# Moving six of eight token transposes from TensorE to DRAM plus VectorE in a Strassen-tiled transformer block

## The chip, the cores and the metric

The kernel runs on one core of one Trainium2 chip, in fp32. The metric is the device time of one execution in microseconds. Three runs of the kernel before gave a median of 853.25 us, from 852.59 to 854.26. The profile was taken from one more execution, which took 852.22 us; its instructions cover a span of 850.4 us.

The engines are named as in the profile: PE is TensorE (PEld its weight loads), DVE is VectorE, ACT is ScalarE, POOL is GpSimd, SP is SyncE, which only issues DMAs here.

## The reference

Four sequences (B = 4) of 512 tokens with 512 features go through two residual blocks. Every `layernorm` is without weights.

```
x = x + layernorm(attn(layernorm(x)))
x = x + layernorm(ffn(layernorm(x)))

attn(x):  i, f, g = x Wi', x Wf', x Wg'            # 512 -> 512 each
          gate = sigmoid(f);  v = silu(i) * (1 - gate)
          o[t] = gate[t] * o[t-1] + v[t]           # a scan over the tokens
          o = rmsnorm(o) * gnorm_w * g * sigmoid(g)
          return o Wo'
ffn(x):   h = silu(x W1') * (x W3')                # 512 -> 2048
          return fwht(h) W2'                       # Hadamard transform, 2048 -> 512
```

The Hadamard transform is applied to W2 instead of to h, once, at the start.

## The kernel before

All large products are done with one level of the Strassen-Winograd scheme: both operands are cut into 2 x 2 blocks, and seven products P1 to P7 of sums of blocks take the place of eight. `ORDER` lists them in the order in which PE runs them: P1, P2, P6, P5, P7, P3, P4. Their results go into three PSUM banks X, Y and Z, and X and Z are added into again by a later product, so a product has to wait until the state that the one before it left in its bank was read out (by ACT, `nc.scalar.copy`, or by DVE, `nc.vector.tensor_add`, in `seven`). One product is 8 matmuls of 128 x 256 columns.

The left operand's sums S1, S2, S4 (S3 takes the place of A21) are made by `combine_left`, the right operand's T1, T2, T4 (T3 in place of B12) by `combine_right`, both on DVE.

The work of a sequence b is

* `normalize(b, "a")`: statistics on DVE, the power -1/2 on POOL, the scaling on ACT (L234); the result `xn` has the tokens on the partitions;
* `transpose(b, "a")`: 16 PE transposes of 128 x 128 with the identity (L281) into four PSUM banks, two copies out by DVE (L288), two by ACT (L286), then `combine_right`; the result `xt` has the features on the partitions and holds the seven right blocks. It is the moving operand of all products with weights;
* three attention units `attn_unit(b, u)`: u = 0 and 1 make half of i and f each and scan; u = 2 makes g and the gated output `og`, a left operand;
* `attn_out(b)`: the product of `og` with Wo (tile y), then the norm of the output, and `normalize` and `transpose` of the new x under the name "f";
* eight FFN units `ffn_unit(b, m)`, 256 hidden features each, and `ffn_out` after every second, which adds into the tile `f`; the last one ends with the output norm.

The order on PE and on SP is the order of the program text, by hand (`tc.manual_schedule`). So that PE never waits for the results of a unit, the products of `attn_out`, `ffn_out` and of the one-time W2 transform are put in a list `fill`, and `run` takes one of them after every product (dense) or after four of the seven. The order on DVE, ACT and POOL is made by a scheduler, which knows priorities: `tc.high_priority(offset=URGENT)` pulls PSUM reads forward, `SOON` is weaker; `behind("P3")` puts work on DVE behind the PSUM read of the last P3.

Weights stream through five buffers (`stream`, w1, w3, wi, wf, wg) and four (`stream2`, wo, w2). In the first sequence each weight tile is read from its input, combined on DVE, used, and written to DRAM with its sums (`kept`, on the POOL queue); later sequences read that back (`again`). Wo is prepared once, by `prepare_wo`: two tiles, four loads on SP (L496), four scalings by `gnorm_w` on DVE (L503), sums, write-back. Its first use is `attn_out(0)`, whose first product is put after P5 of `attn_unit(1, 0)`.

Each SP load waits in the queue for its buffer, for the DMA eight before it, and for what it reads, and everything behind it waits too. The tile `wide` has three buffers, shared by `xn`, `y` and `f`; `xt` has two.

The eight calls of `transpose` stand at these places of the span: (0,"a") at 11.9 us, (1,"a") at 62.3, (0,"f") at 118.0, (2,"a") and (1,"f") together at 281.5, (3,"a") and (2,"f") together at 473.1, (3,"f") at 672.9.

## Time and profile before

| | |
|---|---|
| median of three runs | 853.25 us |
| the profiled execution | 852.22 us, its span 850.4 us |
| PE busy | 825.3 us, 97% of the span |
| PEld, DVE, ACT, POOL busy | 709.5, 453.5, 263.3, 60.6 us |
| transposes on PE (L281) | 128, in groups of 16 that take 1.91 us |
| their PSUM copies on DVE and ACT | 16 and 16, medians 0.68 and 0.59 us |
| DMA | 159.05 MB, 187 GB/s over the span |
| median time to landing, 896 KB weight tile | 6.2 us |

Times in the timeline are from the span's start. A line of the timeline gives the start, the duration, the engine, the source line, the operation, the output and the inputs with their shapes, how many instructions of this kind follow one another, and in brackets how long the engine had been idle and what ended that. A product of 8 matmuls is shown with 1.89 us, but the next one starts 1.73 us after it, since matmuls overlap.

### The profile page before, as it was taken

The numbers are of one execution on the slowest core, as the hardware profiler recorded it, in microseconds if no ns is written. First come the engines' busy times: TensorE is split into PE (matmuls) and PEld (weight loads), VectorE is DVE, ScalarE is ACT, GpSimd is POOL, SyncE is SP. The second block draws the span as 40 slices with busy tenths as digits, with TensorE's granted clock in tenths as the row PEclk, the third lists the DMA queues.
The fourth block names the chain that finished last, engine by engine and source line by source line (L and its number), as shares of the span: only waits on it lengthen the run. The fifth ranks groups of instructions, "written<-read, shape, count | busy, mean of one in ns | idle before, by whom it ended". The sixth has DMA issues, their size and how long they took to land.

```text
span 850.4 us, 9880 instructions
## 1 busy us (share of the span) xinstructions
PE 825.3 (97%) x3808; PEld 709.5 (83%) x3808; DVE 453.5 (53%) x903; ACT 263.3 (31%) x386; POOL 60.6 (7%) x102
## 2 busy tenths in 40 slices
PE   6999989999999999999999999999999999999995
PEld 4778868888888888888888888888888888888884
DVE  6457686755663656537433645737334534633445
ACT  4454362433221225225321222423221211222111
POOL 4110110111110001002000000101000000100000
PEclk9999999999999999999999999999999999999998
DMA  9995376677788224826325222844251632625101
GB/s 315 412 344 212 119 264 231 222 272 272 283 297 304 87 87 158 373 95 240 136 95 209 94 87 93 316 160 174 87 214 44 261 151 110 224 86 217 64 23 49
DMA packets 53598, 159.05 MB, mean 187 GB/s; under 512 B 4272, under 2 KB 29488, under 8 KB 53552
## 3 DMA queue, kind: packets, MB, share of 16 engines
q1 hardware_dynamic: 46544, 121.71, 39.1%
q0 software_dynamic: 7008, 36.71, 10.9%
q8 instruction: 30, 0.49, 0.2%
q14 instruction: 16, 0.13, 0.0%
HBM read 120.66 MB, written 37.75 MB: 186 GB/s over the span
## 4 chain that ended last, share of the span: by engine, by line
PE 59%; issue 9%; DVE 4%; DMA 1%; ACT 1%; POOL 1%; SPq 0%; POOLq 0%; DVEq 0%
PE X_f L333 20%; PE Z_f L333 10%; PE X_po L466 9%; PE Z_po L466 5%; PE Y_f L333 5%; PE X_a L333 3%; PE Y_po L466 2%; PE X_y L419 2%; PE Z_a L333 1%; PE Z_y L419 1%; DMA s_w<-w 1%; PE Y_a L333 1%; DVE x L267 1%; DVE f L318 1%; DMA w<-in_W_dram 1%
## 5 line engine op out<-in xcount | busy, mean ns | idle before, releaser
L333 PE MATMUL X_f<-xt_f,w 128*128 128x256 f32 x1024 | 242.1, 380 | 2.4 <-DVE xt_f L288 1.2
L333 PEld LDWEIGHTS X_f<-xt_f,w 128*128 128x128 f32 x1024 | 193.7, 190 | 33.8 <-issue 3.8
L320 ACT COPY d_f<-X_f 128x512 f32<-128x512 f32 x96 | 56.1, 584 | 300.3 <-PE X_f L333 275.9
L333 PE MATMUL Z_f<-xt_f,w 128*128 128x256 f32 x512 | 121.1, 379 | 0.0
L466 PE MATMUL X_po<-w,ht 128*128 128x256 f32 x512 | 120.9, 379 | 0.2 <-DVE f L318 0.2
L333 PEld LDWEIGHTS Z_f<-xt_f,w 128*128 128x128 f32 x512 | 97.2, 190 | 15.1 <-issue 1.0
L466 PEld LDWEIGHTS X_po<-w,ht 128*128 128x128 f32 x512 | 97.2, 190 | 13.8 <-DVE f L318 0.6
L318 DVE TENSOR_TENSOR f<-X_po,f 128x512 f32<-128x512 f32 x52 | 35.8, 688 | 95.2 <-PE X_po L466 95.2
L348 DVE TENSOR_TENSOR ht<-d_f 128x1024 f32<-128x1024 f32 x32 | 39.1, 1221 | 73.9 <-ACT d_f L442 54.7
L466 PE MATMUL Z_po<-w,ht 128*128 128x256 f32 x256 | 60.6, 379 | 0.5 <-DVE f L318 0.5
L333 PE MATMUL Y_f<-xt_f,w 128*128 128x256 f32 x256 | 60.5, 379 | 0.0
L333 PEld LDWEIGHTS Y_f<-xt_f,w 128*128 128x128 f32 x256 | 48.6, 190 | 8.3 <-issue 1.2
L466 PEld LDWEIGHTS Z_po<-w,ht 128*128 128x128 f32 x256 | 48.6, 190 | 7.5 <-DVE f L318 0.9
L320 ACT COPY d_a<-X_a 128x512 f32<-128x512 f32 x36 | 21.0, 584 | 91.5 <-PE X_a L333 75.4
L214 POOL TENSOR_TENSOR rs_f<-rs_f,power 128x2 f32<-128x2 f32 x16 | 14.6, 915 | 482.3 <-DVE rs_f L211 461.5
L318 DVE TENSOR_TENSOR d_f<-Z_f,d_f 128x512 f32<-128x512 f32 x32 | 22.0, 689 | 26.4 <-PE Z_f L333 26.4
L333 PE MATMUL X_a<-xt_a,wi 128*128 128x256 f32 x128 | 33.3, 382 | 2.1 <-DVE xt_a L288 1.9
L318 DVE TENSOR_TENSOR d_f<-X_f,d_f 128x512 f32<-128x512 f32 x32 | 22.1, 690 | 24.9 <-PE X_f L333 24.9
L442 ACT ACTIVATE d_f<-d_f 128x1024 f32<-128x1024 f32 x32 | 33.8, 1055 | 0.9
L333 PE MATMUL X_a<-xt_a,wf 128*128 128x256 f32 x128 | 32.8, 379 | 0.0
L333 PE MATMUL X_a<-xt_a,wg 128*128 128x256 f32 x128 | 30.7, 382 | 2.3 <-DVE d_a L318 1.6
L318 DVE TENSOR_TENSOR f<-Z_po,f 128x512 f32<-128x512 f32 x28 | 19.3, 689 | 24.4 <-PE Z_po L466 24.4
(148 smaller groups left out, 995.5 us busy)
## 6 DMA issues: line engine op xcount, KB each, us to landing
w<-s_w SPq DMA_DIRECT2D x80, 896.0 KB, 6.2
s_w<-w POOLq DMA_DIRECT2D x24, 896.0 KB, 4.6
w<-in_W_dram SPq DMA_DIRECT2D x32, 256.0 KB, 5.6
wi<-s_wi SPq DMA_DIRECT2D x6, 896.0 KB, 9.4
wf<-s_wf SPq DMA_DIRECT2D x6, 896.0 KB, 6.6
wg<-s_wg SPq DMA_DIRECT2D x6, 896.0 KB, 5.4
wo<-s_wo SPq DMA_DIRECT2D x6, 896.0 KB, 9.3
w2p<-in_W_dram SPq DMA_DIRECT2D x8, 512.0 KB, 7.5
```

The costliest lines, as they stand in the source:

```text
L214: nc.gpsimd.tensor_tensor(r, r, power_t[:, 0:n], ALU.pow)
L267: nc.vector.scalar_tensor_tensor(x_t, y[:, i, t, :], r[:, t : t + 1], x_t, ALU.mult, ALU.add)
L318: read[what] = nc.vector.tensor_add(to, ps[which], to)
L320: nc.scalar.copy(to, ps[which])
L333: nc.tensor.matmul(ps[:, n, :], w[:, a, c, :], xt[:, bb, c, :], start=first and n == 0 and c == 0, stop=c == 1, skip_group_check=True,)
L348: nc.vector.tensor_mul(to.rearrange("p (t k) f -> p k t f", t=2), a.rearrange("p k (t f) -> p k t f", t=2), b2.rearrange("p k (t f) -> p k ...
L419: nc.tensor.matmul(ps[:, t, :], og[:, a, c, ts(t, P)], w[c][:, bb, :], start=first and t == 0 and c == 0, stop=c == 1, skip_group_check=True,)
L442: nc.scalar.activation(d[:, 0], d[:, 0], AF.Silu)
L466: nc.tensor.matmul(ps[:, t, :], hts[b, m][:, a, ts(t, P)], w[m][:, bb, :], start=first and t == 0 and m == ms[0], stop=m == ms[-1], skip_g ...
```

## The change

`normalize_tiles` writes the normalized tokens to DRAM, two token tiles (512 KB) per DMA on the POOL queue, except for (0,"a") and (0,"f"), which keep the transposes on PE. `load_fold` reads them back on the SP queue in four DMAs, each with 128 features of all tokens, to 32 partitions: partition 32 i + q holds, of the tokens 32 g + q, the features 128 i to 128 i + 127. In that layout `transpose_fold` needs only 32 x 32 block transposes: four DVE instructions with 512 elements per partition, each of which reads every fourth element, and then `combine_right` as before. To match, feature 4 p + c goes to partition p, block c; so weight rows are loaded with `(p c)` in place of `(c p)`, and the remaining PE transposes take columns with a step of four. Wo and W2, whose rows are not features of `xn`, stay as they were.

The six moved transposes are also issued earlier in the program: (1,"a") is loaded before `attn_unit(0, 2)` and transposed in it, ahead of `prepare_wo`; (2,"a"), (3,"a") and (3,"f") are loaded before FFN unit 6 and transposed before unit 7; (1,"f") and (2,"f") are loaded before attention unit 1 and transposed before unit 2.

```diff
-                in_=src[:, cols].rearrange("(c p) f -> p c f", p=P),
+                in_=src[:, cols].rearrange("(p c) f -> p c f", p=P),
...
+    ON_TENSOR = ("a", 0), ("f", 0)
...
+        if (name, b) not in ON_TENSOR:
+            if (name, b) not in xnd:
+                xnd[name, b] = scratch.tile(
+                    [NT, P, D], F32, tag=f"xn_{name}_{b}", name=f"xnd_{name}_{b}"
+                )
+            nc.gpsimd.dma_start(
+                out=xnd[name, b][i0 : i0 + n].rearrange("t p d -> p t d"),
+                in_=t[:, i0 : i0 + n, :],
+            )
...
-                    nc.tensor.transpose(pt[c][:, h, ts(i % 2, P)], xn[:, i, ts(c, P)], ident)
+                    nc.tensor.transpose(pt[c][:, h, ts(i % 2, P)], xn[:, i, c::ND], ident)
...
+    def load_fold(b, name):
+        folds[name, b] = t = work.tile(
+            [P, T // 32, P], F32, tag="wide", name=f"fold_{name}_{b}", bufs=3
+        )
+        rows = xnd[name, b].rearrange("t p d -> (t p) d")
+        for i in range(4):
+            nc.sync.dma_start(
+                out=t[ts(i, 32)],
+                in_=rows[:, ts(i, P)].rearrange("(g q) k -> q g k", q=32),
+            )
+
+    def transpose_fold(b, name):
+        fold = folds.pop((name, b)).rearrange("p (h g) k -> p h g k", h=2)
+        xt = work.tile([P, 7, 2, H], F32, tag="xt", name=f"xt_{name}_{b}", bufs=2)
+        with tc.high_priority(offset=SOON):
+            for c in range(ND):
+                to = xt[:, B11 : B12 + 1 : B12 - B11] if c < 2 else xt[:, B21 : B22 + 1]
+                nc.vector.transpose(
+                    to[:, :, c % 2, :].rearrange("p h (g q) -> p h g q", q=32),
+                    fold[:, :, :, c::ND],
+                )
+            combine_right(xt, nc.vector)
+        xts[name, b] = xt
...
     load_attn_w(1, 0)
+    load_fold(1, "a")
     attn_unit(0, 2)
+    with behind("P7"):
+        transpose_fold(1, "a")
     with behind("P3"):
         prepare_wo()
-    transpose(1, "a")
...
+            if m == 6 and not last:
+                load_fold(*((b + 2, "a") if b + 2 < B else (b + 1, "f")))
+            if m == NU - 1 and not last:
+                transpose_fold(*((b + 2, "a") if b + 2 < B else (b + 1, "f")))
             ffn_unit(b, m, b == 0)
...
-            transpose(b + 2, "a")
-            transpose(b + 1, "f")
...
+                if u == 1:
+                    load_fold(b + 1, "f")
+                if u == 2:
+                    transpose_fold(b + 1, "f")
                 attn_unit(b + 2, u)
...
-            transpose(b + 1, "f")
```

More of the change, by code (lines that the diff above doesn't have):

```diff
@@ L216, in scales @@
         return r, nb
-    xns = {}
+    xns, xnd = {}, {}
+    ON_TENSOR = ("a", 0), ("f", 0)
     def normalize_tiles(b, name, i0, n):
@@ L288, in transpose @@
                     nc.vector.tensor_copy(to[:, :, c % 2, :], pt[c])
+            combine_right(xt, nc.vector)
+        xts[name, b] = xt
+    folds = {}
+    def load_fold(b, name):
[18 more added lines that the diff above has]
+                )
             combine_right(xt, nc.vector)
```

## The prediction, made before the changed kernel ran

> **What bounds the kernel now.** I read the page's busy shares and slices first, then the chain, then PE's timeline at the eight transposes.

> ```profile
> PE 825.3 (97%) x3808; PEld 709.5 (83%) x3808; DVE 453.5 (53%) x903; ACT 263.3 (31%) x386; POOL 60.6 (7%) x102
> PE   6999989999999999999999999999999999999995
> DMA  9995376677788224826325222844251632625101
> PE 59%; issue 9%; DVE 4%; DMA 1%; ACT 1%; POOL 1%; SPq 0%; POOLq 0%; DVEq 0%
> ```

> PE bounds every stage after the first 21 us; DMA is full only in the first three slices (to 64 us). So what leaves PE counts in full, unless PE then waits elsewhere. The groups by shape and PE's timeline price the transposes:

> ```profile
> L281 PE MATMUL pt_f<-ident,xn_f 128*128 128x128 f32 x64 | 7.9, 273 | 0.1
> L281 PE MATMUL pt_a<-ident,xn_a 128*128 128x128 f32 x64 | 7.6, 273 | 0.0
> 281.46 1.91 PE L281 MATMUL pt_a<-ident,xn_a 128*128 128x128 f32 x16
> 283.21 1.91 PE L281 MATMUL pt_f<-ident,xn_f 128*128 128x128 f32 x16
> 284.96 1.03 PE L333 MATMUL X_a<-xt_a,wi 128*128 128x256 f32 x4
> ```

> One transpose takes PE 283.21 - 281.46 = 1.75 us, and here nothing more. At 62 us it also waits for copies, and there DVE is busy with Wo (mixed timeline):

> ```profile
> 61.37 0.87 DVE L503 TENSOR_SCALAR wo<-wo,gn 128x512 f32<-128x512 f32 x2
> 62.28 1.91 PE L281 MATMUL pt_a<-ident,xn_a 128*128 128x128 f32 x16
> 62.48 0.59 ACT L320 COPY d_a<-X_a 128x512 f32<-128x512 f32 x1 [4.59 <-PE X_a L333]
> 63.10 1.91 ACT L375 ACTIVATE d_a<-d_a 128x2048 f32<-128x2048 f32 x1
> 64.72 1.28 DVE L288 COPY xt_a<-pt_a 128x512 f32<-128x512 f32 x2
> 65.46 1.13 PE L333 MATMUL X_a<-xt_a,wi 128*128 128x256 f32 x4 [1.26 <-DVE xt_a L288]
> 72.47 1.89 PE L419 MATMUL X_y<-wo,og 128*128 128x256 f32 x8
> ```

> [...] the four Wo loads, 256 KB in 1 KB rows, beside POOL's 7 KB rows:

> ```profile
> DMA to landing us min/median/max: 3.8/11.3/12.7
> ```

> **What leaves.** Of the moved places, (2,a)+(1,f) frees 3.50 us; (3,a)+(2,f), 473.13 to 476.98, 3.85; (3,f), 672.87 to 675.53 plus 0.10 of a slow restart, 2.76. Sum 10.1 us. (1,a), 62.28 to 65.46, held PE 3.18; it is taken below. The 24 PSUM copies (0.68 DVE, 0.59 ACT) were off the path but for the waits in these gaps.

> **What comes: transposes.** 24 on DVE, 512 elements each, no such row in the trace. Lower bound: the rate of the copy, L288, 0.60 start to start. But the source steps by four elements[...]. My estimate is 0.96 apart; ends 0.60 and 1.36. PE's remaining two transposes load weights with that step:[...] I take 0.7.

> **What comes: DMAs.** 12 POOL writes of 512 KB (`w_h<-w2p`, the same size, lands in 6.9 us) and 24 SP loads of 256 KB in 512-byte rows; 2 MB per transpose. [...] Five folds are hidden. Behind the load that precedes each in the queue there is: (2,a), loads end at 242.5, DVE reaches the transposes at 258.2, 15.7 us; (1,f) 299.8 to 316.9, 17.1; (3,a) 434.5 to 451.6, 17.1; (2,f) 493.6 to 510.7, 17.1; (3,f) 634.2 to 651.3, 17.1. Preceding load (6.2) plus fold (4.8) is 11. Without that cover DVE would stand, with PSUM reads behind it, and PE one product later. The POOL writes wait for ACT; power steps queue behind them, at 0.5 us each, and their norms are not due yet. From 205 to 255 us DMA is at 0.6 to 0.8, and 3 MB more costs nothing by my reading; up to 2 us if wrong.

> **The first one, (1,a).** xn is ready at 46.6 (ACT L234, 45.10 + 1.52), the second write lands about 50.5, and only then SP issues the fold, with the four Wo loads (before: 48.3) and wi behind it. From 45 to 60 POOL and SP owe 4.3 + 1.4 MB in large packets at 370 GB/s: 60.4. Then the fold,[...] it lands at 64 (ends 61.4, 68). DVE is free from 61.4 and waits; in the built program's order the og product, Y's PSUM read and the Wo work stand behind. Four transposes to 67.8, T1 to 68.4, then og. Before, og could not start before 65.0 either (ACT L375 ends 65.01). So og is 3.4 late.

> The built order also puts Wo behind og. From og's start to the first scaling of the second Wo tile come og 1.13, T2, Y, T3, T4 0.60 each, og 1.13, scaling 0.41, S1 0.60, scaling 0.42, S2, S3, S4 0.60, o 1.13, sum 0.34, o 0.60, three sums 1.1, scaling 0.5, and about 0.4 for dependent pairs: 11.95 us. (Spacings from the timeline of 64.7 to 72.) With y's first product behind P5, before at 72.47, PE waits until 65.05 + 3.4 + 11.95 = 80.4, less 0.2 for its first matmul: **7.7 us lost** net, the freed 3.18 included. With the fold at 61.4 and 0.60 per transpose it is still 77.0 - 72.6 = 4.4.

> **The wait at (1,f).** There the final norm of sequence 0 keeps DVE busy, and `combine_right` comes too (4 x 0.60). Before:

> ```profile
> 326.85 2.33 DVE L368 TENSOR_TENSOR_SCAN o<-d_a 128x512 f32<-128x512 f32 x2
> 328.82 1.99 PE L333 MATMUL X_a<-xt_a,wg 128*128 128x256 f32 x8 [0.43 <-ACT d_a L320]
> 332.38 1.89 PE L333 MATMUL X_a<-xt_a,wg 128*128 128x256 f32 x8
> ```

> In the new order at 0.60 apart: transposes, the two PSUM reads and T1 to T4 to 323.5; statistics; the gate (L363) 324.7; second Y 325.9; norms to 328.8; scans to 331.3; four x updates (0.65) to 333.9; the read of P7 to 334.5. P4 needs that read: 334.55 instead of 332.38, 2.2 late; with 0.96, 4 x 0.36 = 1.4 more: **3.6 us lost**. At (2,f) `ffn_out` products lie between, and the same count leaves P7 its read 2 us early: nothing. At unit 7 DVE is idle 2.7 to 4.5 us at a time.

> **Sum.** -10.1 + 7.7 + 3.6 + 0.7 = +1.9. The span becomes 852.3, the execution (1.8 around it) 854.1; the median of before is 1.0 above its profiled execution, so **855.1 us**.

> **Rivals.**
> *Faster.* DVE takes the step of four at full rate (0.60) and the fold lands by 61.4: losses 4.4 + 2.2, no slow weight loads: -3.5, 849.8. For it: the copies from PSUM run at that rate. Against: the full DMA slices[...]. With the fold at 61.4 all else as worked, it decides at a spacing near 1.05; at 64, near 0.72.
> *The two waits don't bind*, because DVE's order leaves slack that I count as used: -10.1 plus about 2: 845. Against: both come from instruction orders that are fixed.
> *Slow transposes*, 1.36 apart: 9.3 + 5.2 + 0.7 - 10.1 = +5.1, 858.4; at 2.3 apart[...] about 866. Nothing in the profile excludes it.
> *DMA in sequence 0* turns late with 3 MB more: up to 2 us on top, 857. The change cannot fail to happen: 96 PE transposes are absent from the built program.

> **Chances.** As worked 0.42, the faster rival or half of it 0.22, no binding waits 0.13, slow transposes 0.19, DMA 0.04. The likeliest's own range is 852 to 858. The range 849 to 863 leaves out the 845 case and the worst of slow transposes. What a measurement of this kernel can tell is 0.2%, 1.7 us: faster than 851.5 has 0.13 + 0.13 + a little of the first, 0.30; within, 0.24; slower, 0.46.

> **What would show it.** Right: no L281 at 281, 473 and 673, PE stalls there gone; a PE wait of some 7 to 10 us near 70 us released by DVE `wo`, one of 2 to 4 near 332 released by `d_a`; the DVE transpose at 0.9 to 1.1 us; the (1,a) fold landing near 64. Wrong: transposes near 0.68, no wait before X_y, or waits of DVE for a fold at the five later places.

## The result and the profile after

The changed kernel takes 860.35 us (median of 6 runs, 858.92 to 864.81). Against the kernel before on the same chip (853.1) the ratio is 1.0084, with an interval from 1.0065 to 1.0103: slower by 0.8%, inside the range given, on the side held likeliest, but by 7 us where 2 were forecast. The profiled execution took 859.53 us, its span 857.8 against 850.4.

The lines of the page that answer to those shown of before (busy shares, slices, shares of the chain):

```profile
PE 820.3 (96%) x3712; PEld 702.1 (82%) x3712; DVE 469.9 (55%) x915; ACT 257.0 (30%) x374; POOL 69.7 (8%) x114
PE   6985999999999999999999999999999999999994
PEclk9997999999999999999999999999999999999998
PE 83%; DVE 7%; DMA 5%; issue 2%; ACT 1%; SPq 1%; POOL 1%; POOLq 0%; DVEq 0%
```

PE still bounds the kernel nearly everywhere. The exceptions are slices 3 and 4, 43 to 86 us: PE is busy for 8 and 5 tenths, and the clock that TensorE was granted (row PEclk, in tenths of full speed) falls to 7 tenths in slice 4. Before, that row had no digit below 9 until the last slice. PE's waits, as total, times and longest:

```profile
PE X_y L463 <- DVE wo L547: 5.6, 1, 5.6
PE X_a L377 <- issue: 5.4, 1, 5.4
PE X_a L377 <- DVE d_a L362: 3.5, 3, 1.7
```

The mixed timeline of PE and DVE shows the first two:

```profile
60.70 1.89 PE L377 MATMUL X_a<-xt_a,wg 128*128 128x256 f32 x8
66.77 4.01 DVE L329 STREAM_TRANSPOSE xt_a<-fold_a 128x512 f32<-128x512 f32 x4 [5.18 <-DMA fold_a<-xnd_a]
67.96 2.15 PE L377 MATMUL X_a<-xt_a,wi 128*128 128x256 f32 x4 [5.37 <-issue]
71.25 1.24 DVE L392 TENSOR_TENSOR og<-o,d_a 128x1024 f32<-128x1024 f32 x1
74.65 0.69 DVE L362 TENSOR_TENSOR d_a<-Y_a,d_a 128x512 f32<-128x512 f32 x1 [1.56 <-PE Y_a L377]
78.13 0.70 PE L463 MATMUL X_y<-wo,og 128*128 128x256 f32 x2
84.41 2.93 PE L463 MATMUL X_y<-wo,og 128*128 128x256 f32 x6 [5.58 <-DVE wo L547]
```

First the fold is late, and PE and DVE both stand (the profile puts PE's wait down to "issue"; its first matmul follows the end of the first DVE transpose, 67.86, by 0.1 us). SP could issue the fold's loads only at 54.67, when the second write had landed:

```profile
54.67 5.13 SPq L316 DMA_DIRECT2D fold_a<-xnd_a  x4
```

Four transposes then take 4.01 us on DVE, 0.98 apart by the start of the next instruction (70.68), and `og` and Wo queue behind them. At 84.41 PE goes on in the middle of y's first product, when the second Wo tile is scaled. The shapes show something more: half a product, four matmuls, takes 2.15 and 1.91 us after the first wait, and 1.03 in normal running. The same stretch in windows (columns: stretch, its length, busy us of PE, PEld, DVE, ACT and POOL, granted clock, DMA share, GB/s):

```profile
66.00:68.00 2.00, 0.04 (x1) 0.07 (x1) 1.23 (x2) 0.00 (x0) 0.00 (x0) 0.72 1.08 384
72.00:74.00 2.00, 2.00 (x7) 1.59 (x6) 1.09 (x2) 0.44 (x1) 0.00 (x0) 0.57 1.04 430
80.00:82.00 2.00, 0.00 (x0) 0.00 (x0) 2.00 (x4) 0.09 (x1) 0.00 (x0) 0.63 0.00 0
86.00:88.00 2.00, 2.00 (x8) 1.65 (x7) 0.21 (x1) 0.58 (x1) 0.53 (x1) 0.66 0.91 380
```

The stretches between 68 and 72 and from 82 to 86 have 0.50. So the clock was halved twice: a mean of 0.72 over 2 us is 1.12 us at half, that is from 66.9; the other three give its end near 73.7, a second fall near 80.5 and an end near 87.4.

Where the 7.3 us of span come from, as the delay of each matmul against the same matmul of before, with PE's transposes left out of the comparison:

| place (before, us) | delay before and after it | change |
|---|---|---|
| start, to 62 | 0 to 0.15 | +0.15 |
| (1,a): fold late, PE idle (65.46) | to 2.50 | +2.35 |
| (1,a): half clock (to 68.4) | to 5.36 | +2.86 |
| y's first product waits for Wo (72.9) | to 11.51 | +6.15 |
| half clock after it (to 74.4) | to 13.05 | +1.54 |
| (2,a), (1,f) gone (284.96) | 13.22 to 9.72 | -3.50 |
| (1,f) on DVE: PE's three waits (329 to 333) | 9.62 to 12.60 | +2.98 |
| y's next product waits for a load of Wo (350) | 12.60 to 13.11 | +0.51 |
| (3,a), (2,f) gone (476.98) | 13.11 to 9.26 | -3.85 |
| (3,f) gone (675.53) | 9.30 to 6.53 | -2.77 |
| after the last output has landed | 1.63 to 2.40 us of span | +0.77 |

What is left of the sum, 0.1, are drifts below 0.2. PE's three waits at (1,f):

```profile
338.48 1.99 PE L377 MATMUL X_a<-xt_a,wg 128*128 128x256 f32 x8 [0.47 <-ACT d_a L364]
341.19 1.99 PE L377 MATMUL Z_a<-xt_a,wg 128*128 128x256 f32 x8 [0.71 <-ACT d_a L364]
344.88 1.99 PE L377 MATMUL X_a<-xt_a,wg 128*128 128x256 f32 x8 [1.69 <-DVE d_a L362]
```

### The profile page after: what moved, and what is told of

It is laid out like the page before. It is cut to its first block, busy times and chain, and to the rows that moved or that the text cites. A ratio compares the mean times of both kernels' runs of the same rounds, so it can differ in the third digit from the quotient of the medians.

```text
span 857.8 us, 9759 instructions
## 1 busy us (share of the span) xinstructions
PE 820.3 (96%) x3712; PEld 702.1 (82%) x3712; DVE 469.9 (55%) x915; ACT 257.0 (30%) x374; POOL 69.7 (8%) x114
## 3 DMA queue, kind: packets, MB, share of 16 engines
q0 software_dynamic: 8736, 43.01, 12.7%
## 4 chain that ended last, share of the span: by engine, by line
PE 83%; DVE 7%; DMA 5%; issue 2%; ACT 1%; SPq 1%; POOL 1%; POOLq 0%; DVEq 0%
PE X_f L377 24%; PE Z_f L377 12%; PE X_po L510 12%; PE X_a L377 7%; PE Z_po L510 6%; PE Y_f L377 6%; PE Z_a L377 3%; PE X_y L463 3%; PE Y_po L510 3%; PE Y_a L377 2%; PE Z_y L463 2%; PE g L601 2%; DMA wg<-in_Wg_dram 2%; DMA wo<-s_wo 1%; PE h L572 1%
## 5 line engine op out<-in xcount | busy, mean ns | idle before, releaser
L510 PE MATMUL Z_po<-w,ht 128*128 128x256 f32 x256 | 60.6, 379 | 0.6 <-DVE f L362 0.6
L463 PE MATMUL X_y<-wo,og 128*128 128x256 f32 x128 | 32.2, 394 | 6.0 <-DVE wo L547 5.6
L377 PEld LDWEIGHTS X_a<-xt_a,wi 128*128 128x128 f32 x128 | 24.6, 196 | 13.7 <-issue 8.9
```

What stands on the lines that cost most here:

```text
L377: nc.tensor.matmul(ps[:, n, :], w[:, a, c, :], xt[:, bb, c, :], start=first and n == 0 and c == 0, stop=c == 1, skip_group_check=True,)
L463: nc.tensor.matmul(ps[:, t, :], og[:, a, c, ts(t, P)], w[c][:, bb, :], start=first and t == 0 and c == 0, stop=c == 1, skip_group_check=True,)
L510: nc.tensor.matmul(ps[:, t, :], hts[b, m][:, a, ts(t, P)], w[m][:, bb, :], start=first and t == 0 and m == ms[0], stop=m == ms[-1], skip_g ...
```

## The experiments

Each was timed against the kernel before on the same chip; that one's median was 854.22 us beside the runs with (1,a) alone on TensorE, 11 and 12 dummies, Wo first and neighbouring elements, 853.37 beside the last three runs below, and 853.93 beside the other four. Executions differ by about 2 us already at the start: PE's first products wait about 1 us for W2, and in 6 of the 13 profiled executions, that of the row order alone among them, those after it run at half speed too (in the kernel before, four matmuls take 3.56 us ahead of that wait and 1.99 behind it; from 4 to 16 us PE has 30 matmuls there and 22 with the row order alone). Where spans are compared below, this is named. Every statement about a wait is read from one profiled execution of its run.

**(1,a) back on TensorE.**

```diff
-    ON_TENSOR = ("a", 0), ("f", 0)
+    ON_TENSOR = ("a", 0), ("f", 0), ("a", 1)
...
-    load_fold(1, "a")
     attn_unit(0, 2)
-    with behind("P7"):
-        transpose_fold(1, "a")
     with behind("P3"):
         prepare_wo()
+    transpose(1, "a")
```

> Only the first moved transpose, (1,a), goes back to TensorE at its old place; the other five stay on DVE. Theory (nearly all of the loss sits at this one site: fold late 2.4 us, half clock after it 2.9, wait for Wo 5.9, half clock after that 1.5, in all 12.9 of the span of 857.8): span 844.9, ratio to before 0.993 (0.992 to 0.995), no slice of low clock between 60 and 90 us. Rival (the traffic of 12 writes and 24 loads and the new row order cost time everywhere): span stays above 849, ratio 0.998 or more.

Measured: 848.04 us, ratio 0.9923 (0.9908 to 0.9938), span 845.1. From 66 to 90 us the clock is whole and PE never stands:

```profile
66.00:76.00 10.00, 10.00 (x48) 8.81 (x47) 10.00 (x17) 4.05 (x5) 0.00 (x0) 1.00 0.52 219
76.00:90.00 14.00, 14.00 (x70) 12.42 (x70) 6.73 (x12) 5.28 (x7) 0.53 (x1) 1.00 0.49 170
```

So the loss is this one site's: without it the change gains 0.8%. The other five freed places and the waits at (1,f) stay as they were.

**PE kept busy in the two waits.** To tell an idle PE from a busy memory, dummy matmuls fill the waits.

```diff
+    def keep_busy(n, name):
+        p = bank(name)
+        for _ in range(n):
+            nc.tensor.matmul(p, h_sb, xs[0][:, 0, :], start=True, stop=True)
...
     while len(fill) > 1:
         slot()
-    fill.extend([None] * 3 + attn_out(0))
+    keep_busy(11, "busy0")
+    steps = attn_out(0)
+    fill.extend([None] * 3 + [lambda: (keep_busy(12, "busy1"), steps[0]())] + steps[1:])
```

> The changed kernel, and in its two long PE waits 11 and 12 matmuls of 128x512 (0.43 us each) whose result nobody reads: PE is busy while it waits, and waits no less. Theory (the PE clock halves because PE stood idle): matmuls after both waits run at 1.73 us per product, 2.9 + 1.5 us less, span 853.4, ratio 1.0033 (1.002 to 1.005); X_y still starts near 81 or 82 us. Rival (the matmuls after the waits are slow because DMA and DVE use the same memory): granted clock or product spacing as in the changed kernel, ratio 1.008.

Measured: 870.16 us, ratio 1.0200 (1.0171 to 1.0229). My price of the dummy was wrong: each is two records of 0.43 us, so 9.6 and 10.5 us were spent in waits of 5.4 and 5.6. The time says nothing; the clock does: it is whole from 8.9 us to the last slice (0.995 over the span). A second form has 5 and 8 in place of 11 and 12:

> As the run with busy PE, with 5 and 8 of the matmuls of 128x512 in place of 11 and 12, since each takes 0.86 us (two records of 0.43) and they ran past the end of the waits. Theory (idle PE halves its clock): no half clock after either wait, the first product near 68 as in the changed kernel; the Y read then no longer holds DVE up by 1.6 us, so X_y goes on near 82.8 in place of 84.4, and 1.5 us of half clock behind it are gone: span 854.7, ratio 1.005 (1.0035 to 1.0065). Rival (memory contention): products after the waits 3.4 us apart in spite of the busy PE, ratio 1.008.

Measured: 860.89 us, ratio 1.0076 (1.0063 to 1.0089). Its windows, which had a clock of 0.72, 0.50 and 0.63 in the changed kernel, and PE's timeline:

```profile
66.00:68.00 2.00, 2.00 (x6) 0.95 (x5) 0.00 (x0) 1.07 (x1) 0.00 (x0) 1.00 1.16 216
70.00:72.00 2.00, 1.73 (x7) 1.22 (x8) 2.00 (x3) 0.00 (x0) 0.00 (x0) 1.00 1.04 438
80.00:82.00 2.00, 2.00 (x6) 0.95 (x5) 2.00 (x4) 0.45 (x1) 0.00 (x0) 1.00 0.00 0
```

```profile
71.41 1.03 PE L382 MATMUL X_a<-xt_a,wf 128*128 128x256 f32 x4
78.77 7.03 PE L340 MATMUL busy<-x,had 128*128 128x512 f32 x16
85.64 1.89 PE L468 MATMUL X_y<-wo,og 128*128 128x256 f32 x8
```

The clock is whole through both waits, and half a product takes 1.03 us while DMA runs at 1.04 of its share beside it (70 to 72). The rival, contention, falls. On DVE nothing waits for Y any more. From `og` to the scaling of the second Wo tile, first in the changed kernel (12.61 us), then with 5 and 8 dummies (10.96):

```profile
71.25 1.24 DVE L392 TENSOR_TENSOR og<-o,d_a 128x1024 f32<-128x1024 f32 x1
83.86 0.89 DVE L547 TENSOR_SCALAR wo<-wo,gn 128x512 f32<-128x512 f32 x2
73.26 1.23 DVE L397 TENSOR_TENSOR og<-o,d_a 128x1024 f32<-128x1024 f32 x1
84.22 0.89 DVE L552 TENSOR_SCALAR wo<-wo,gn 128x512 f32<-128x512 f32 x2
```

So half clock after the first wait had made this chain 1.65 us longer. The time missed its expectation: this execution lost 2.1 us at the start, the last dummy ran past the scaling of Wo by about a microsecond, and another wait near 248 (below) was 1.3 longer. Start taken off, the delay at X_y is 13.17 - 2.06 = 11.1 us, against 13.05 - 0.15 = 12.9 behind X_y in the changed kernel: 1.8 of the 3.1 expected. That an idle PE halves the clock, and what this does to the chain on DVE, is shown; what a cure would bring in time is not.

**Wo first.** Its loads go ahead of the fold's on SP, its scaling and sums ahead of the transposes on DVE.

```diff
     load_attn_w(1, 0)
+    load_wo()
     load_fold(1, "a")
     attn_unit(0, 2)
-    with behind("P7"):
-        transpose_fold(1, "a")
-    with behind("P3"):
+    with behind("P3"), tc.high_priority(offset=URGENT):
         prepare_wo()
+    with behind("P3"):
+        transpose_fold(1, "a")
```

> The changed kernel with the four Wo loads ahead of the fold's loads on SP and the scaling and sums of Wo ahead of the transposes on DVE, as before the change. Theory (5.9 us of the wait at X_y, and 1.5 of half clock behind it, come from Wo's place behind og): no wait at X_y over 1 us, while the first wait and its half clock stay and grow by 0 to 2 us, since the fold's loads are now behind 1 MB of Wo; span 850.4 to 852.4, ratio 1.000 to 1.002. Rival (X_y waits for og and the transposes' queue on DVE anyway): a wait of 4 us or more before X_y, ratio 1.006 or more.

Measured: 856.94 us (19 runs, 853.47 to 861.01), ratio 1.0039 (1.0027 to 1.0051). The profiled execution was the shortest of them, span 851.7:

```profile
70.72 2.16 PE L377 MATMUL X_a<-xt_a,wi 128*128 128x256 f32 x4 [8.36 <-issue]
79.26 1.89 PE L463 MATMUL X_y<-wo,og 128*128 128x256 f32 x8
```

X_y no longer waits: Wo's place made that wait, and the rival falls. It was the place on DVE more than that on SP, since in the changed kernel Wo had landed by 69.0 and its first scaling began at 77.59. The first wait grew to 8.4 us, more than allowed for, with the fold behind 1 MB of Wo. The span of this execution lies where it was expected, but the median is 3.5 above it, and the ratio expected, 1.000 to 1.002, was missed. The granted clock, 0.992 in the profiled execution and 0.986 to 0.991 in the others, suggests that half clock lasts longer in most of them; their traces are not there to show it.

**Neighbouring elements.** What does the step of four cost? The features then reach the products in another order, so the result is not that of the reference; sizes and counts are the same.

```diff
-                    fold[:, :, :, c::ND],
+                    fold[:, :, :, ts(c, 32)],
```

> The changed kernel with each DVE transpose reading 32 neighbouring elements in place of every fourth (the features come out in another order, so the products use permuted features; sizes and counts are the same). Theory (the step of four is what makes a transpose 0.98 us): 0.60 us apart; 0.4 less before the first product at 68 us, 1.1 to 1.5 less before X_y, 1.5 less at 330 to 345; span 854.4, ratio 1.0044 (1.003 to 1.006). Rival (a 32x32 block transpose of fp32 has this price for any source): 0.98 us apart, ratio 1.008.

Measured: 858.46 us, ratio 1.0052 (1.0034 to 1.0070). The instruction itself, minimum, median and maximum in ns, and the last wait at (1,f):

```profile
L329 DVE STREAM_TRANSPOSE xt_f<-fold_f x12: 667/668/702, 330.9 to 665.1; 128x512 f32<-128x512 f32 x12
347.52 1.99 PE L377 MATMUL X_a<-xt_a,wg 128*128 128x256 f32 x8 [1.70 <-DVE d_a L362]
```

0.67 us where the step of four took 1.09 to 1.12, and 0.60 apart: the step is the price. Of (1,f)'s waits 1.7 us remain, the two for ACT are gone. The 0.3% gained agrees with the expectation, and is only just clear of noise.

**(1,f).** Three ways to ease it, all with (1,a) on TensorE: on TensorE too; on DVE with neighbouring elements, ACT writing them in that order; and moved one attention unit earlier, without and with ACT's reordering.

```diff
# on TensorE: for b == 0, after load_attn_w(b + 2, 0)
+                transpose(b + 1, "f")
# ACT's order: the scaling's output and input
+                to = to.rearrange("p (i c k) -> p i c k", i=4, c=ND)
+                x_k = x_k.rearrange("p (i k c) -> p i c k", i=4, c=ND)
# earlier
-                if u == 1:
+                if u == 0:
                     load_fold(b + 1, "f")
-                if u == 2:
+                if u == 1:
                     transpose_fold(b + 1, "f")
```

> (1,a) and (1,f) on TensorE at their old places, four on DVE. Theory ((1,f) on DVE costs 0.8 + 2.0 + 0.5 us of waits from 329 to 350, on TensorE 1.75): 1.5 us under the run with (1,a) alone on TensorE, 846.5, ratio 0.9905 (0.989 to 0.992), no PE wait over 1 us from 320 to 350. Rival (the waits come from the output norm, not from the transposes on DVE): waits stay, 849.8, ratio 0.9945.

Measured: 846.03 us, ratio 0.9915 (0.9901 to 0.9928). No wait over 1 us from 320 to 350: the transposes on DVE make the waits, not the output norm. The time cannot be told from that with (1,a) alone on TensorE (0.9923).

> (1,a) on TensorE; the other five with ACT writing the normalized tokens in such an order that the DVE transpose reads 32 neighbouring elements, all features where they belong. Theory: 0.60 us apart as with permuted features, the waits at (1,f) fall from 2.8 + 0.5 to near 1.1: 1.9 under the run with (1,a) alone on TensorE, 846.2, ratio 0.990 (0.9885 to 0.992); ACT's scaling, 0.81 us, keeps its duration. Rival (the step of four now costs on ACT, at 1.3 us or more, and delays the writes): ratio 0.9925 or more.

Measured: 849.79 us, ratio 0.9953 (0.9941 to 0.9965), a miss. ACT's scaling grew from 0.81 to 1.32 us (the 1.19 of the next expectations is a mean with those left as they were), and PSUM reads queue behind it: new PE waits of 0.9 at 174.6 and 1.7 at 408.4. The rival was right: the step of four costs on ACT too, and there it is on PE's path.

> As the run before, and the folds of (1,f) and (2,f) are loaded and transposed one attention unit earlier, where DVE is idle 2 to 3.5 us at a time. Theory (the waits at (1,f) come from where on DVE the transposes stand): no wait over 1 us from 300 to 350 us, 3 us under the run with (1,a) alone on TensorE, 845.0, ratio 0.9885 (0.987 to 0.990). Rival (DVE is late there anyway, and the waits move to unit 1): a wait of 1 us or more from 300 to 330, ratio 0.990 or more.

Measured: 849.24 us, ratio 0.9944 (0.9932 to 0.9956), a miss too. No wait over 1 us from 300 to 350, as the theory had it, but ACT's two waits are there (1.0 and 1.7). So the move was tried with ACT as it was:

> (1,a) on TensorE, transposes on DVE with the step of four as in the change (ACT as before), and the folds of (1,f) and (2,f) loaded and transposed one attention unit earlier. Theory (place alone makes the waits at (1,f); ACT's longer scaling, 1.19 in place of 0.81 us, took the gain back in the run before, with waits of 1.1 us at 175 and 1.9 at 409): no PE wait over 1 us from 300 to 350, at 175 and at 409; 3.3 us under the run with (1,a) alone on TensorE, span 842 to 843, ratio 0.989 (0.9875 to 0.9905). Rival (at 1.1 us each the transposes hold up reads in unit 1): a wait of 1 us or more from 300 to 330, ratio 0.991 or more.

Measured: 845.39 us (843.87 to 849.64), ratio 0.9915 (0.9894 to 0.9937), span 842.5. PE's timeline where the three waits were:

```profile
324.53 1.89 PE L377 MATMUL Z_a<-xt_a,wg 128*128 128x256 f32 x8
326.84 1.99 PE L377 MATMUL X_a<-xt_a,wg 128*128 128x256 f32 x8 [0.42 <-ACT d_a L364]
328.67 1.89 PE L377 MATMUL Z_a<-xt_a,wg 128*128 128x256 f32 x8
330.40 1.89 PE L377 MATMUL X_a<-xt_a,wg 128*128 128x256 f32 x8
```

The span is as expected and the waits are gone. The median gained less, its interval just short of the 0.989 of the theory, and it cannot be told from the run with (1,f) on TensorE, nor from that with (1,a) alone: that the place of the transposes makes the waits is shown, that moving them saves time is not.

**The wait near 235.** PE waits there for a DVE read that stands behind weights: 0.5 us before and 0.6 after, but 1.3 to 2.2 in the profile of every other run above. Moving the normalization of sequence 2, and so its two writes, by one unit:

> As the run before, and sequence 2 is normalized (and written to DRAM) one FFN unit later, at unit 5 of sequence 0. Theory (the two writes of 512 KB ahead of W2 rows and weights make DVE wait for weights, and PE behind it 1.5 to 2.3 us near 235, against 0.7 in the kernel before): that wait falls to 0.9 or less, about 1 us gained, ratio 0.988, unless the fold for unit 7 lands late. Rival (the reordered weight rows load more slowly): the wait stays at 1.5 or more, same ratio as the run before.

Measured: 846.09 us, ratio 0.9908 (0.9895 to 0.9922). The wait is still 1.4: the moved writes land at 229.6 and 233.2, among the same loads. And the row order alone:

```diff
-                in_=src[:, cols].rearrange("(c p) f -> p c f", p=P),
+                in_=src[:, cols].rearrange("(p c) f -> p c f", p=P),
...
-                    nc.tensor.transpose(pt[c][:, h, ts(i % 2, P)], xn[:, i, ts(c, P)], ident)
+                    nc.tensor.transpose(pt[c][:, h, ts(i % 2, P)], xn[:, i, c::ND], ident)
```

> The kernel before with only the new order of the weight rows and with the step of four in all eight TensorE transposes; nothing goes through DRAM, nothing moves to DVE. Theory (the strided weight loads, 209 ns in place of 141, are hidden by the overlap of transposes, and the rows load as fast): ratio 1.000 (0.998 to 1.002), wait near 233 of 0.7 us. Rival (the row order slows the weight loads): wait of 1.5 us or more near 233, ratio 1.002 to 1.005. Rival (the strided loads cost 0.07 us per transpose of 128x128[...]): 8 us, ratio 1.010.

Measured: 854.45 us (22 runs), ratio 1.0011 (1.0003 to 1.0019). The wait is 0.7, near that of before, so the row order does not make it. That the writes do is argued (1 MB more in a stretch where DMA is full, at a share of 1.00 to 1.02 from 215 to 230 us in the run with the folds earlier), since moving them did not end it. The strided weight loads take 209 ns for 141, and the delay grows by 0.33 and 0.32 us at the two double transposes, 0.16 for each, and not at the three single ones behind the start, where PE waits for copies anyway.

## Why the prediction was right, and where it was not

* **What leaves**: forecast 3.50 + 3.85 + 2.76, measured 3.50 + 3.85 + 2.77. Work that leaves an engine which bounds its stage counts in full, and its start-to-start gap prices it.
* **Transposes on DVE**: forecast 0.96 apart, measured 0.98; with neighbouring elements 0.60, the rate of the copy that was the lower bound. The 0.96, and the 1.36 of the rival with slow transposes, were my estimates: the trace of before has no transpose on DVE.
* **The wait at (1,f)**: forecast 3.6, measured 3.0, partly by other reads than the one named: two of the waits (0.5 and 0.7) are for ACT, whose copies stand behind the norm's work, and only the last for P7's read. The delay grew by 3.5 there because y's product at 350 also waited for a load of Wo, which the runs with (1,a) alone on TensorE and with neighbouring elements do not show: that the sum comes so near is luck.
* **Five hidden folds**: right; no DVE wait for a fold after the first. A fold ends 4.3 to 4.8 us after the landing of the load ahead of it, where 4.8 was an estimate that no trace of before showed, and 9.1 to 10.3 after its own first issue, inside the cover of 15.7 to 17.1.
* **Strided weight loads**: forecast 0.7, an estimate that no trace of before showed; measured nothing above 0.2, though one takes 209 ns for 141. **Writes from 205 to 255**: forecast nothing; 0.1 in the profiled execution, about 1 us in most of the other kernels with these writes. If the writes make it, which is argued above, this is the rival of a late DMA in sequence 0, at half its size.
* **(1,a)**: forecast 7.7, measured 12.9. This is the step that failed, in two terms. *The fold's landing*: 66.6 for 64, since the second write, issued at 47.05, took 7.55 us and landed at 54.6, where the working had 50.5; so `og` started at 71.25, not 68.4, 2.8 late. *The clock*: the working priced PE's waits but not what they do to PE. Half clock after the first wait delayed Y's product, for whose read DVE stood 1.56 us (with PE kept busy it did not stand), so the chain from `og` to the second Wo tile took 13.2 us for 11.95 (1.2 more); half clock after the second wait cost 1.5. Together 5.5, less 0.3 of smaller differences.
* **Left out**: 0.8 us after the last output, 0.15 at the start.

That the time lies inside 849 to 863 is partly luck. The likeliest account's own range, 852 to 858, was missed, and the room above it was given for slow transposes and a late DMA, not for the clock.

Of the rivals, the faster one fell on both conditions, and the two waits did bind. The slow transposes, at 858.4, had nearly the right time for a wrong reason.

The clock should have been in the working. The trace of before shows it fall once, at the end, after PE's last matmuls, which end at 840.26 (PE's timeline, then two windows):

```profile
838.37 1.89 PE L466 MATMUL X_po<-w,ht 128*128 128x256 f32 x8
841.00:844.00 3.00, 0.00 (x0) 0.00 (x0) 2.52 (x9) 1.33 (x2) 1.01 (x2) 1.00 0.01 5
845.00:848.00 3.00, 0.00 (x0) 0.00 (x0) 1.41 (x2) 0.94 (x2) 0.00 (x0) 0.50 0.48 184
```

The clock is whole until 844.9, 4.6 us after them. And the forecast itself had PE idle from 62 to about 65 and again for several microseconds before X_y. How short a wait can do it, no trace of before shows. In the changed kernel the first fall came after 4.3 us without PE, 62.6 to 66.9, the second after only 1.7, 78.8 to 80.5, and the two stretches at half clock, to 73.7 and to 87.4, last 6.8 us each (the last section has more).

## What to carry to other kernels

When work moves off the bounding engine through a longer path, ask of each place whether the path has cover there: by the waits in the profiles, five of six moves were worth their transposes, or could be made so, and the one without cover lost more than all gained. Price a wait of TensorE at more than its length where it can halve the clock: here products after such waits ran at half clock for up to 6.8 us, and work on other engines that reads them was late too. By the shares in the last section, an estimate, a wait from about 1.8 us on (54% of a step of 3.41) can do so, depending on where it falls, and one over 3.7 us, twice that, wherever it falls. The strided access that left DVE turned up on ACT; such an access belongs on an engine with slack at that place.

## What the runs showed of the hardware

```profile
77.12:80.53 3.41, 1.57 (x7) 0.72 (x5) 3.41 (x7) 2.38 (x2) 0.00 (x0) 1.00 0.00 0
246.47:249.88 3.41, 1.25 (x7) 0.93 (x6) 3.17 (x9) 0.58 (x1) 0.53 (x1) 1.00 0.13 52
73.75:77.16 3.41, 1.71 (x8) 1.15 (x7) 3.41 (x7) 1.30 (x1) 0.00 (x0) 1.00 0.11 44
330.34:333.75 3.41, 1.71 (x8) 1.18 (x8) 3.09 (x5) 0.00 (x0) 2.21 (x4) 1.00 0.52 208
```

So a wait of 2.2 us was followed by half clock where it lay in one step, and waits of 2.6 and 2.8 us were not where they lay across two. Full clock came back after every step at half clock with PE busy for 84% or more, and after none with 80% or less. This fits the changed kernel, which had two steps at half clock after its first wait: PE was busy for 2.33 us, 68%, of the first of them.

* The span goes on after the last output has landed for 1.63 us without any transposes through DRAM (two kernels), 2.08 with four, 2.23 with five (five kernels), 2.40 with six (the changed kernel and four others): about 0.13 us for each, that is for six more DMAs. The cause is open.
